# Linear attention's scores and values in blocks of 64 keys, with two heads stacked on the 128 rows

## The chip, the core and the metric

The kernel runs on one core of a Trainium2 chip. The metric is the time of one execution on the device in microseconds (us); a median of several runs is given with its lowest and highest. The profile is one further execution, taken by the hardware profiler.

## The reference, cut to what matters

Eight sequences of 1024 rows and 256 features go through four residual stages: linear attention with its own MLP, an MLP with relu, softmax attention, and an MLP whose operands are rounded to FP4 blocks. All is float32. The change lies in the first stage, for 16 heads of 16 features:

```python
q = sigmoid(heads(Wq, bq)); k = sigmoid(heads(Wk, bk)); v = heads(Wv, bv)
# flows: sink_in, src_comp, sink_alloc, from running sums of q and k
qs = q * (sink_in / normal)[..., None]
vs = v * src_comp[..., None]
kv = cumsum(einsum('bhld,bhlm->bhldm', k, vs), axis=2)
x = einsum('bhld,bhldm->bhlm', qs, kv) * sink_alloc[..., None]
attn = x @ Wo + bo
```

The kernel doesn't form the running sum of outer products for every row. For a chunk of 128 rows it computes, for each head, the scores of all its keys against all its queries, keeps those where the key doesn't come after the query, multiplies them with `vs`, and adds what all earlier chunks give through one 16x16 sum per head, `kv_sum`. Then it adds this chunk's own k times vs to that sum.

## The kernel before, in words

**Groups and chunks.** The rows are 64 chunks of 128 (`P`), four to a group (`G`), 16 groups, two to a sequence. `linear_group` (L970) does a group's layer norms (`front`, L980), and `linear_span` (L1023) its projections to q and k (feature rows by 512 positions), the running sums, and the per-head factors; `comp` holds the factor for v. `linear_chunk` (L1185) does the rest of one chunk: v, scores, values, output projection, layer norm. `dense` (L1388) runs both MLPs a group behind, `soft_chunk` (L1556) the softmax attention and the FP4 MLP, a sequence behind.

**Order of the work.** All of these are generators, run by a small planner (`Plan`, L67). It estimates when every engine and tile would be free (`took`, L164), picks the next part by readiness and priority (`run`, L310), and fixes the order of the instructions on each engine when the program is built. On the chip every engine works through its list in that order and waits on semaphores. `took` prices a matmul by its columns, and at a quarter of that if it uses a 32-row or 32-column tile of the array. Where the planner expects a long pause of TensorE it puts in matmuls of the identity (`fill`, L1710). A transposition (`flip`, L651) goes to TensorE if the planner expects it to have little to do (`idle`, L295), otherwise through a copy on POOL (`cut`), a DMA transpose on SP's queue (`spun`) and a copy on ACT.

**One chunk of linear attention.** The q tile has features on the 128 rows, as two halves k of eight heads. TensorE's array is used as four tiles of 32 rows, r = 0 to 3, with two heads in each, an even and an odd one. ACT makes two copies of the chunk's queries, `qz` (L1233), times `parity[:, e]`, which is 1 on the features of even (e = 0) or odd heads and 0 on the others. A score matmul (L1249) has 128 keys as weights, 32 rows deep, and streams the 256 columns of both copies; there are eight, into four PSUM banks of 512 columns. DVE multiplies each bank by the 0/1 triangle `triu` (L1266) into `sc`; in group 0 (`by_act`), TensorE first puts large negative numbers into the bank from the bf16 tile `later` (L1240), and ACT takes a relu.

For the values (L1306), the weights are 32 columns of `pad`: one of four zeroed tiles `v_pads` (L483), where DVE has written vs with zeros between, so that the 16 columns of one head sit beside 16 zero columns (`v_columns`, L847). Sixteen matmuls stream 128 columns of `sc` each, on four tiles of 32 array columns, and add up in one bank. Ahead of them, from the second chunk of a sequence on, eight matmuls of `kv_sum` with q (L1295) go to the same bank. After them come eight of `kT` with the chunk's vs (L1321), 32 columns each, whose result DVE and POOL add to `kv_sum`.

**Conditions.** The v of chunk c may start when fewer than `V_PADS` = 4 chunks before it are unattended (L1194). The next group's `linear_group` starts when all v's of this group have started (L1000), and each of its fronts when fewer than `RES` = 10 residual tiles are in use (L983). `qz` of chunk c waits until fewer than two chunks before it are unattended (L1226). The next group's q and k wait until this group's four chunks are through the output projection (L1047).

Of the kernel before, what the change touches and what calls it, by code (L numbers as in the profile page):

```python
# [9 lines left out]
F32 = mybir.dt.float32  # L10
# [3 lines left out]
AF = mybir.ActivationFunctionType  # L14
ALU = mybir.AluOpType
AX = mybir.AxisListType

P = 128
D = 256
H = 16  # L20
DH = D // H
FF = 1024
NF = FF // P
INTER = 704
V_PADS = 4
W_FF = 2
IDLE = 1, 0.0
RES = 10
# [4 lines left out]
GT = G * P  # L33
# [12 lines left out]
    "x": (4, D, F32),  # L46
    "n0": (2, D, F32),
    "lin": (4, D, F32),
    "flow": (8, 512, F32),
    "xr": (2, D, F32),  # L50
    "norm": (3, D, F32),
# [15 lines left out]
class Plan:  # L67
# [197 lines left out]
    def pe(self, *tiles, **kw):  # L265
        return self.need("tensor", tiles, **kw)

    def dve(self, *tiles, **kw):
        return self.need("vector", tiles, **kw)

    def act(self, *tiles, **kw):
        return self.need("scalar", tiles, **kw)
# [102 lines left out]
def block_stack_kernel(ctx: ExitStack, tc: tile.TileContext, a: dict, out: bass.AP):  # L375
# [20 lines left out]
    plan = Plan(tc, tc.nc)  # L396
    nc, pe, dve, act, dma = plan, plan.pe, plan.dve, plan.act, plan.dma
    x_dram = a["L0_attn_inputs"]
    B, L, _ = x_dram.shape
# [3 lines left out]
    const = ctx.enter_context(tc.tile_pool(name="const", bufs=1))  # L403
    big = ctx.enter_context(tc.tile_pool(name="big", bufs=1))
    wk = ctx.enter_context(tc.tile_pool(name="wk", bufs=2))
    sm = ctx.enter_context(tc.tile_pool(name="sm", bufs=4))
# [6 lines left out]
    def mm_bank():  # L413
        bank = ps.tile([P, 512], F32, tag="bank", name="bank")
        plan.bank(bank)
        return bank
# [4 lines left out]
    def fresh(kind, need, name=None):  # L421

        need.fresh = kind
        yield need
        return make(kind, name)
# [51 lines left out]
    make_identity(tc.nc, ident)  # L477
    bdiag = const.tile([P, P], F32, name="bdiag")
    make_block_diagonal(tc.nc, bdiag, DH)
    triu = const.tile([P, P], F32, name="triu")  # L480
    make_upper_triangular(tc.nc, triu)

    v_pads = [const.tile([P, H, 32], F32, name=f"v_pad{i}") for i in range(V_PADS)]  # L483
    for v in v_pads:
        nc.vector.memset(v, 0.0)
    neghalf = const.tile([P, 1], F32, name="neghalf")
# [18 lines left out]
    parity = const.tile([P, 2], F32, name="parity")  # L505
# [10 lines left out]
    later = make("q_c", "later")[:, : GT + P]  # L516
# [18 lines left out]
    def late_constants():  # L535
        yield dve(at=0.05)
        nc.vector.tensor_reduce(
            parity, bdiag.rearrange("p (g e d) -> p e g d", e=2, d=DH), AX.XY, ALU.max
        )
        nc.vector.memset(hsum, 0.0)  # L540
        for b in range(4):
            yield dve()
            nc.vector.tensor_copy(
                hsum[:, b, 8 * b : 8 * b + 8], bdiag.rearrange("p (h d) -> p h d", d=DH)[:, :, 0]
            )
        late.add("hsum")
        yield dve(triu)
        nc.vector.tensor_scalar(
            later[:, :GT].rearrange("p (n t) -> p n t", n=4),
            triu.unsqueeze(1).to_broadcast([P, 4, P]),  # L550
            -1.0,
            2.0**100,
            ALU.add,
            ALU.mult,
        )
        yield dve()
        nc.vector.tensor_reduce(
            same[:, 0, :], ident.rearrange("p (t r) -> p r t", r=32), AX.X, ALU.add
        )
        for g in range(NG):  # L560
            yield dve()
            nc.vector.reciprocal(rpos[:, g, :], pos[:, g, :])
        nc.vector.memset(front, 0.0)
        for t in range(1, G):
            yield dve()
            nc.vector.tensor_copy(same[:, t, :], same[:, 0, :])
            nc.vector.tensor_copy(front[: 32 * t, t, :], same[: 32 * t, 0, :])
        late.add("positions")
# [136 lines left out]
    def two(t):  # L705
        return t.rearrange("p (k t) -> p k t", k=2)
# [137 lines left out]
        plan.drop(*turns)  # L844
        weights.add("softmax")

    def v_columns(v, pairs):  # L847

        return bass.AP(
            tensor=v.tensor,  # L850
            offset=v.offset + 64 * pairs.start,
            ap=[list(v.ap[0]), [64, len(pairs)], [64 - DH, 2], [1, DH]],
        )

    weights = set()

# [328 lines left out]
    def linear_chunk(p, i, n0T, comp, qk):  # L1185
# [4 lines left out]
        here = slice(i * P, (i + 1) * P)  # L1190
        yield pe(
            n0T,
            banks=1,
            when=lambda: count["v"] == c and c - count["attended"] < V_PADS and "v" in late,  # L1194
        )
        bank = mm_bank()
        for k in range(2):
            nc.tensor.matmul(
                bank[:, :D],
                lhsT=n0T[:, k, here],  # L1200
                rhs=wqkv[2][:, k, :],
                start=k == 0,
                stop=k == 1,
            )
        count["v"] += 1
        pad = v_pads[c % V_PADS]
        v = yield from fresh("lin", dve(bank), "v")
        nc.vector.tensor_tensor(v, bank[:, :D], bv1, ALU.add)
        yield dve(comp)
        nc.vector.tensor_tensor(  # L1210
            v_columns(pad, range(H // 2)),
            v.rearrange("p (j e d) -> p j e d", e=2, d=DH),
            comp[:, i, H:].rearrange("p (j e) -> p j e", e=2).unsqueeze(3)
            .to_broadcast([P, H // 2, 2, DH]),
# [1 line left out]
        )  # L1216
        plan.drop(v)

        tile_qz = yield from fresh(
            "flow",  # L1220
            act(
                qk[0],
                at=at + 0.62 + 0.06 * i,
                when=lambda: i in groups[p]["scaled"]
                and count["scored"] == c
                and c - count["attended"] < 2,  # L1226
            ),
            "qz",
        )
        count["scored"] += 1  # L1230
        qz = tile_qz.rearrange("p (k e t) -> p k e t", k=2, e=2)
        by_act = p == 0
        for e in range(2):  # L1233
            nc.scalar.activation(
                qz[:, :, e, :], qk[0][:, :, here], AF.Copy, scale=parity[:, e : e + 1]
            )

        yield pe(qz, *([later] if by_act else []), banks=4, tiled=not by_act)
        banks = [mm_bank() for _ in range(4)]
        for bank in banks:  # L1240
            if by_act:
                nc.tensor.matmul(
                    bank, lhsT=later[:, GT:], rhs=later[:, :GT], start=True, stop=False,
                    skip_group_check=True,
                )
        for r, bank in enumerate(banks):
            rows = slice(32 * r, 32 * r + 32)
            for k in range(2):
                nc.tensor.matmul(  # L1249
                    bank[:, k * D : (k + 1) * D],  # L1250
                    lhsT=qk[1][rows, k, here],
                    rhs=qz[rows, k, :, :],
                    start=not by_act,
                    stop=True,
                    skip_group_check=True,
                )
        plan.drop(tile_qz)
        scores = []
        for bank in banks:
            sc = yield from fresh("flow", (act if by_act else dve)(bank), "sc")  # L1260
            sc = sc.rearrange("p (n t) -> p n t", n=4)
            if by_act:
                nc.scalar.activation(sc, bank.rearrange("p (n t) -> p n t", n=4), AF.Relu)
                scores.append(sc)
                continue
            nc.vector.tensor_tensor(  # L1266
                sc,
                bank.rearrange("p (n t) -> p n t", n=4),
                triu.unsqueeze(1).to_broadcast([P, 4, P]),
                ALU.mult,  # L1270
            )
            scores.append(sc)
        end = g == NG - 1 and i == G - 1
        if not end:
# [4 lines left out]
        kv = past.get("kv")  # L1279
        yield pe(  # L1280
            pad,
            *scores,
            *([] if kv is None else [kv]),
            *([] if end else [kT]),
            banks=1,
            tiled=True,
            when=lambda: count["attended"] == c,
        )
        kv = past.get("kv")
# [4 lines left out]
        bank = both[:, :D]  # L1294
        for k in range(2):  # L1295
            for r in range(4):
                if kv is not None:
                    nc.tensor.matmul(
                        bank[32 * r : 32 * r + 32, k * P : (k + 1) * P],
                        lhsT=kv[:, k, 32 * r : 32 * r + 32],  # L1300
                        rhs=qk[0][:, k, here],
                        start=k == 0,
                        stop=False,
                        skip_group_check=True,
                    )
        for k in range(2):  # L1306
            for e in range(2):
                for r in range(4):
                    nc.tensor.matmul(
                        bank[32 * r : 32 * r + 32, k * P : (k + 1) * P],  # L1310
                        lhsT=pad[:, 8 * k + 2 * r + e, :],
                        rhs=scores[r][:, 2 * k + e, :],
                        start=kv is None and k == 0 and e == 0,
                        stop=k == 1 and e == 1,
                        skip_group_check=True,
                    )
        plan.drop(*scores)
        if not end:

            kvbank = both[:, D : D + 64].rearrange("p (k d) -> p k d", k=2)  # L1320
            for k in range(2):  # L1321
                for r in range(4):
                    nc.tensor.matmul(
                        kvbank[32 * r : 32 * r + 32, k, :],
                        lhsT=kT[:, k, 32 * r : 32 * r + 32],
                        rhs=v_columns(pad, range(4 * k + r, 4 * k + r + 1)),
                        start=False,
                        stop=True,
                        skip_group_check=True,
                    )  # L1330
            plan.drop(kT)
        xo = two((yield from fresh("lin", act(bank), "xo")))
        nc.scalar.copy(xo, two(bank))
        if not end:
# [21 lines left out]
        bank = mm_bank()  # L1356
# [8 lines left out]
        h = yield from layernorm_affine("lin", u, ln1g, ln1b)  # L1365
# [398 lines left out]
```

## Time and profile before

| what | value |
| --- | --- |
| median of 3 runs (lowest to highest) | 2563.58 us (2563.43 to 2565.26) |
| the profiled execution's own time | 2562.25 us |
| its span, from the first to the last instruction | 2560.5 us |
| TensorE matmuls busy, share of the span | 2485.7 us, 97% |
| TensorE weight loads busy | 1914.5 us, 75% |
| VectorE (DVE) busy | 2022.4 us, 79% |
| ScalarE (ACT) busy | 1339.4 us, 52% |
| GpSimd (POOL) busy | 1045.1 us, 41% |
| score matmuls (bank<-qz,k) busy, rows | 75.7 us, 1024 |
| value matmuls (bank<-sc,v_pad) busy, rows | 67.9 us, 2048 |

The page of the profile gives busy time by engine and the granted clock; other views give groups of instructions by tile and shape (busy us, mean ns of one, idle before them and who ended it), waits, stretches of time, and a timeline. PE is the matmul row of TensorE, PEld its weight loads. Nearly every instruction stands at line 356, the helper through which the planner issues it, so groups are told apart by their tiles: `out<-in`, rows by elements. A float32 matmul appears as two rows, since the hardware makes two passes. DMA transposes and loads are issued by SP.

### The profile page before, as it was taken

To read this page: it belongs to the slowest core of one execution; us is meant where nothing else is said; L and a number is where in the kernel's file an instruction comes from. 1 tells how busy PE (TensorE), PEld (TensorE's weight loads), DVE (VectorE), ACT (ScalarE), POOL (GpSimd) and SP (SyncE) were. 2 spreads that over 40 slices of the span, in tenths; PEclk is the share of its full clock that TensorE was granted. 3 is DMA by queue.
4 is the path that set the end of the run, shared out by engine and by line. 5 is a ranking of instruction groups with operands and counts; after the bars stand their busy time and mean duration, and the time that the engine had idled before them with its cause. 6 is when DMAs were issued, how large, how long until landed. Compare 5 with 4: busy or idle time off the path is not lost. (4 is left out here: it accounts for less than half of the span.)

```text
span 2560.5 us, 45339 instructions
## 1 busy us (share of the span) xinstructions
PE 2485.7 (97%) x15685; PEld 1914.5 (75%) x15685; DVE 2022.4 (79%) x4416; ACT 1339.4 (52%) x2722; POOL 1045.1 (41%) x1788
## 2 busy tenths in 40 slices
PE   8999999999999999999999999999999999999998
PEld 7777777777877677777777777777777777777767
DVE  6787787887978788796987978688795977866687
ACT  4534546456464645555556564644546456454453
POOL 2433344452534425353453534434443452433222
PEclk9999999999999999999999999999999999999999
DMA  3445555645555554554545554645555444454322
GB/s 88 119 114 148 124 137 126 150 97 125 129 123 133 115 136 108 122 133 110 137 118 121 131 127 120 130 118 120 132 115 119 128 109 116 106 130 117 73 48 62
DMA packets 586821, 301.96 MB, mean 118 GB/s; under 512 B 390240, under 2 KB 575072, under 8 KB 586592
## 3 DMA queue, kind: packets, MB, share of 16 engines
q1 hardware_dynamic: 586592, 299.07, 48.5%
q8 instruction: 124, 2.03, 0.4%
q14 instruction: 105, 0.86, 0.1%
HBM read 188.17 MB, written 20.71 MB: 82 GB/s over the span
## 5 line engine op out<-in xcount | busy, mean ns | idle before, releaser
L356 PE MATMUL bank<-half,w_in 128*128 128x256 f32 x2048 | 531.5, 383 | 14.5 <-ACT half L356 7.0
L356 PE MATMUL bank<-w_out,hidden 128*128 128x256 f32 x2048 | 531.1, 385 | 7.5 <-DMA w_out<-in_L_attn_W_dram 5.0
L356 PEld LDWEIGHTS bank<-w_out,hidden 128*128 128x128 f32 x2048 | 376.0, 191 | 110.7 <-issue 58.2
L356 PEld LDWEIGHTS bank<-half,w_in 128*128 128x128 f32 x2048 | 385.2, 191 | 93.1 <-issue 16.1
L356 POOL TENSOR_SCALAR ln_ve<-ln_mv 128x1 f32<-128x1 f32 x384 | 97.8, 255 | 851.8 <-DVE ln_mv L356 838.5
L356 PE MATMUL bank<-n2T,qT 128*128 128x512 f32 x512 | 243.0, 597 | 5.3 <-ACT qT L356 5.2
L356 POOL TENSOR_TENSOR ln_rstd<-ln_ve,neghalf 128x1 f32<-128x1 f32 x384 | 234.8, 611 | 32.0
L356 ACT ACTIVATE hidden<-bank,c_L_ffn_b 128x256 f32<-128x256 f32 x256 | 120.9, 473 | 241.4 <-PE bank L356 240.6
L356 ACT ACT_TABLE_LOAD x173 | 222.0, 1283 | 25.1 <-DVE nmax L356 19.3
L356 PE MATMUL bank<-vt,probT 128*128 128x256 f32 x1024 | 232.2, 379 | 0.7 <-ACT probT L356 0.7
L356 POOL COPY cut<-prob 128x512 uint16<-128x512 uint16 x211 | 154.5, 751 | 176.7 <-ACT prob L356 110.5
L356 PEld LDWEIGHTS bank<-vt,probT 128*128 128x128 f32 x1024 | 194.0, 190 | 32.3 <-ACT probT L356 2.3
L356 ACT ACTIVATE hidden<-bank,c_L_attn_b 128x256 f32<-128x256 f32 x256 | 119.3, 469 | 168.1 <-PE bank L356 167.7
L356 POOL COPY cut<-n 128x512 uint16<-128x512 uint16 x199 | 146.2, 739 | 121.1 <-DVE n L356 100.4
L356 ACT COPY probT<-spun 128x512 uint16<-128x512 uint16 x223 | 147.4, 675 | 90.6 <-DMA spun<-cut 88.8
L356 PE MATMUL bank<-wgT,xqT 128*128 128x352 f32 x512 | 177.1, 469 | 16.3 <-ACT xqT L356 15.8
L356 PE MATMUL bank<-wdT,hqT 128*128 128x256 f32 x768 | 176.7, 379 | 1.8 <-ACT hqT L356 1.3
L356 PE MATMUL bank<-wuT,xqT 128*128 128x352 f32 x512 | 173.7, 462 | 0.0
L356 PEld LDWEIGHTS bank<-wdT,hqT 128*128 128x128 f32 x768 | 144.9, 190 | 23.3 <-ACT hqT L356 2.1
L356 POOL COPY cut<-hid 128x512 uint16<-128x512 uint16 x156 | 106.9, 707 | 127.7 <-DVE hid L356 93.6
L356 DVE TENSOR_TENSOR sc<-bank,triu 128x512 f32<-128x512 f32 x240 | 149.9, 678 | 8.8 <-PE bank L356 8.6
L356 PEld LDWEIGHTS bank<-n2T,qT 128*128 128x128 f32 x512 | 96.0, 191 | 80.6 <-issue 61.0
(236 smaller groups left out, 4686.8 us busy)
## 6 DMA issues: line engine op xcount, KB each, us to landing
w_in<-in_L_attn_W_dram SPq DMA_DIRECT2D x128, 256.0 KB
w_out<-in_L_attn_W_dram SPq DMA_DIRECT2D x128, 256.0 KB
w_in<-in_L_ffn_w_dram SPq DMA_DIRECT2D x128, 256.0 KB
w_out<-in_L_ffn_w_dram SPq DMA_DIRECT2D x128, 256.0 KB
spread<-packed SPq DMA_DIRECT2D x90, 256.0 KB
spun<-cut SPq DMA_TRANSPOSE x687
x<-in_L_attn_inputs_dram SPq DMA_DIRECT2D x64, 128.0 KB
xr<-in_L_attn_inputs_dram SPq DMA_DIRECT2D x64, 128.0 KB
```

Source lines behind the costliest of these rows:

```text
L356: ins = method(*args, **kw)
```

## The change

The keys of a chunk are cut in two blocks b of 64. The parity mask goes on the keys: ACT writes `kz`, in which the 64 keys of the even head and the same 64 keys of the odd head stand side by side as 128 weight columns. A score matmul streams q itself: all 128 queries for block 0, and the last 64 for block 1, since the first 64 queries come before every key of block 1. So there are 16 score matmuls, of 128 or 64 columns, and a bank holds twice 192 columns instead of 512. The mask `tri` has the same form. The result has two heads' keys on the 128 rows, so vs has to stand likewise in `pad`: DVE writes vs to a tile of its own, `vs`, and POOL and ACT copy it from there in two 64-row pieces each (`into_pad`). Sixteen value matmuls stream 128 or 64 columns. There are two pads instead of four, so L1194's condition becomes fewer than two. The k times vs matmuls read `vs`. Within the score matmuls the loops change order, so that the four row tiles come innermost. The planner's prices for all this follow by its rules, and with them its choices elsewhere.

```diff
@@ -22,7 +22,9 @@
 FF = 1024
 NF = FF // P
 INTER = 704
-V_PADS = 4
+V_PADS = 2
+HB = P // 2
+SCW = P + HB
 W_FF = 2
 IDLE = 1, 0.0
 RES = 10
@@ -46,6 +48,7 @@
     "x": (4, D, F32),
     "n0": (2, D, F32),
     "lin": (4, D, F32),
+    "vs": (V_PADS, D, F32),
     "flow": (8, 512, F32),
     "xr": (2, D, F32),
     "norm": (3, D, F32),
@@ -477,10 +480,16 @@
     make_identity(tc.nc, ident)
     bdiag = const.tile([P, P], F32, name="bdiag")
     make_block_diagonal(tc.nc, bdiag, DH)
-    triu = const.tile([P, P], F32, name="triu")
+    triu = sm.tile([P, P], F32, tag="div", name="triu", bufs=1)
     make_upper_triangular(tc.nc, triu)
-
-    v_pads = [const.tile([P, H, 32], F32, name=f"v_pad{i}") for i in range(V_PADS)]
+    tri = const.tile([P, SCW], F32, name="tri")
+    nc.gpsimd.memset(tri[:, HB:P], 1.0)
+    for e in range(2):
+        h = slice(e * HB, (e + 1) * HB)
+        for c0 in (0, P):
+            nc.gpsimd.tensor_copy(tri[h, c0 : c0 + HB], triu[h, h])
+
+    v_pads = [const.tile([P, 2, H // 2, 32], F32, name=f"v_pad{i}") for i in range(V_PADS)]
     for v in v_pads:
         nc.vector.memset(v, 0.0)
     neghalf = const.tile([P, 1], F32, name="neghalf")
@@ -544,10 +553,10 @@
                 hsum[:, b, 8 * b : 8 * b + 8], bdiag.rearrange("p (h d) -> p h d", d=DH)[:, :, 0]
             )
         late.add("hsum")
-        yield dve(triu)
+        yield dve(tri)
         nc.vector.tensor_scalar(
-            later[:, :GT].rearrange("p (n t) -> p n t", n=4),
-            triu.unsqueeze(1).to_broadcast([P, 4, P]),
+            later[:, : 2 * SCW].rearrange("p (k n) -> p k n", k=2),
+            tri.unsqueeze(1).to_broadcast([P, 2, SCW]),
             -1.0,
             2.0**100,
             ALU.add,
@@ -844,13 +853,9 @@
         plan.drop(*turns)
         weights.add("softmax")
 
-    def v_columns(v, pairs):
-
-        return bass.AP(
-            tensor=v.tensor,
-            offset=v.offset + 64 * pairs.start,
-            ap=[list(v.ap[0]), [64, len(pairs)], [64 - DH, 2], [1, DH]],
-        )
+    def pair_columns(v, j):
+
+        return v.rearrange("p (e j d) -> p j e d", e=2, d=DH)[:, j]
 
     weights = set()
 
@@ -1206,9 +1211,9 @@
         pad = v_pads[c % V_PADS]
         v = yield from fresh("lin", dve(bank), "v")
         nc.vector.tensor_tensor(v, bank[:, :D], bv1, ALU.add)
-        yield dve(comp)
+        vs = yield from fresh("vs", dve(comp))
         nc.vector.tensor_tensor(
-            v_columns(pad, range(H // 2)),
+            vs.rearrange("p (e j d) -> p j e d", e=2, d=DH),
             v.rearrange("p (j e d) -> p j e d", e=2, d=DH),
             comp[:, i, H:].rearrange("p (j e) -> p j e", e=2).unsqueeze(3)
             .to_broadcast([P, H // 2, 2, DH]),
@@ -1216,59 +1221,76 @@
         )
         plan.drop(v)
 
-        tile_qz = yield from fresh(
+        def into_pad(copy, e, b):
+            copy(
+                pad[e * HB : (e + 1) * HB, b, :, e * DH : (e + 1) * DH],
+                vs[b * HB : (b + 1) * HB, e * P : (e + 1) * P].rearrange(
+                    "p (j d) -> p j d", d=DH
+                ),
+            )
+
+        yield plan.pool(vs)
+        for e in range(2):
+            into_pad(nc.gpsimd.tensor_copy, e, e)
+        yield act(vs)
+        for e in range(2):
+            into_pad(nc.scalar.copy, e, 1 - e)
+
+        tile_kz = yield from fresh(
             "flow",
             act(
-                qk[0],
+                qk[1],
                 at=at + 0.62 + 0.06 * i,
                 when=lambda: i in groups[p]["scaled"]
                 and count["scored"] == c
                 and c - count["attended"] < 2,
             ),
-            "qz",
+            "kz",
         )
         count["scored"] += 1
-        qz = tile_qz.rearrange("p (k e t) -> p k e t", k=2, e=2)
+        kz = tile_kz.rearrange("p (k b e t) -> p k b e t", k=2, b=2, e=2)
         by_act = p == 0
         for e in range(2):
             nc.scalar.activation(
-                qz[:, :, e, :], qk[0][:, :, here], AF.Copy, scale=parity[:, e : e + 1]
+                kz[:, :, :, e, :],
+                qk[1][:, :, here].rearrange("p k (b t) -> p k b t", b=2),
+                AF.Copy,
+                scale=parity[:, e : e + 1],
             )
-
-        yield pe(qz, *([later] if by_act else []), banks=4, tiled=not by_act)
-        banks = [mm_bank() for _ in range(4)]
+        kz = tile_kz.rearrange("p (k b n) -> p k b n", k=2, b=2)
+
+        yield pe(tile_kz, qk[0], *([later] if by_act else []), banks=4, tiled=not by_act)
+        banks = [mm_bank()[:, : 2 * SCW] for _ in range(4)]
         for bank in banks:
             if by_act:
                 nc.tensor.matmul(
-                    bank, lhsT=later[:, GT:], rhs=later[:, :GT], start=True, stop=False,
+                    bank, lhsT=later[:, GT:], rhs=later[:, : 2 * SCW], start=True, stop=False,
                     skip_group_check=True,
                 )
-        for r, bank in enumerate(banks):
-            rows = slice(32 * r, 32 * r + 32)
-            for k in range(2):
-                nc.tensor.matmul(
-                    bank[:, k * D : (k + 1) * D],
-                    lhsT=qk[1][rows, k, here],
-                    rhs=qz[rows, k, :, :],
-                    start=not by_act,
-                    stop=True,
-                    skip_group_check=True,
-                )
-        plan.drop(tile_qz)
+        for k in range(2):
+            for b in range(2):
+                for r, bank in enumerate(banks):
+                    rows = slice(32 * r, 32 * r + 32)
+                    nc.tensor.matmul(
+                        bank[:, k * SCW + b * P : k * SCW + P + b * HB],
+                        lhsT=kz[rows, k, b, :],
+                        rhs=qk[0][rows, k, i * P + b * HB : (i + 1) * P],
+                        start=not by_act,
+                        stop=True,
+                        skip_group_check=True,
+                    )
+        plan.drop(tile_kz)
         scores = []
         for bank in banks:
             sc = yield from fresh("flow", (act if by_act else dve)(bank), "sc")
-            sc = sc.rearrange("p (n t) -> p n t", n=4)
+            sc = sc[:, : 2 * SCW].rearrange("p (k n) -> p k n", k=2)
+            bank = bank.rearrange("p (k n) -> p k n", k=2)
             if by_act:
-                nc.scalar.activation(sc, bank.rearrange("p (n t) -> p n t", n=4), AF.Relu)
-                scores.append(sc)
-                continue
-            nc.vector.tensor_tensor(
-                sc,
-                bank.rearrange("p (n t) -> p n t", n=4),
-                triu.unsqueeze(1).to_broadcast([P, 4, P]),
-                ALU.mult,
-            )
+                nc.scalar.activation(sc, bank, AF.Relu)
+            else:
+                nc.vector.tensor_tensor(
+                    sc, bank, tri.unsqueeze(1).to_broadcast([P, 2, SCW]), ALU.mult
+                )
             scores.append(sc)
         end = g == NG - 1 and i == G - 1
         if not end:
@@ -1279,6 +1301,7 @@
         kv = past.get("kv")
         yield pe(
             pad,
+            vs,
             *scores,
             *([] if kv is None else [kv]),
             *([] if end else [kT]),
@@ -1304,14 +1327,14 @@
                         skip_group_check=True,
                     )
         for k in range(2):
-            for e in range(2):
+            for b in range(2):
                 for r in range(4):
                     nc.tensor.matmul(
-                        bank[32 * r : 32 * r + 32, k * P : (k + 1) * P],
-                        lhsT=pad[:, 8 * k + 2 * r + e, :],
-                        rhs=scores[r][:, 2 * k + e, :],
-                        start=kv is None and k == 0 and e == 0,
-                        stop=k == 1 and e == 1,
+                        bank[32 * r : 32 * r + 32, k * P + b * HB : (k + 1) * P],
+                        lhsT=pad[:, b, 4 * k + r, :],
+                        rhs=scores[r][:, k, b * P : P + b * HB],
+                        start=kv is None and k == 0 and b == 0,
+                        stop=k == 1 and b == 1,
                         skip_group_check=True,
                     )
         plan.drop(*scores)
@@ -1323,12 +1346,13 @@
                     nc.tensor.matmul(
                         kvbank[32 * r : 32 * r + 32, k, :],
                         lhsT=kT[:, k, 32 * r : 32 * r + 32],
-                        rhs=v_columns(pad, range(4 * k + r, 4 * k + r + 1)),
+                        rhs=pair_columns(vs, 4 * k + r),
                         start=False,
                         stop=True,
                         skip_group_check=True,
                     )
             plan.drop(kT)
+        plan.drop(vs)
         xo = two((yield from fresh("lin", act(bank), "xo")))
         nc.scalar.copy(xo, two(bank))
         if not end:
```

## The prediction, made before the result was known

> **What bounds the kernel now.** I read the page first: busy time by engine and the granted clock.
>
> ```profile
> PE 2485.7 (97%) x15685; PEld 1914.5 (75%) x15685; DVE 2022.4 (79%) x4416; ACT 1339.4 (52%) x2722; POOL 1045.1 (41%) x1788
> PEclk9999999999999999999999999999999999999999
> ```
>
> TensorE's matmul row is busy 2485.7 of 2560.5 us, at full clock: 74.8 us are idle. Busy can flatter (ends are modelled), so next the table by stretches and the waits.
>
> ```profile
> 0.00:320.00 320.00, 295.06 (x2346) 236.41 (x2347) 242.03 (x574) 148.70 (x342) 110.16 (x207) 0.98 0.44 119
> 320.00:2240.00 1920.00, 1878.35 (x11984) 1441.64 (x11983) 1550.28 (x3322) 1037.04 (x2062) 837.88 (x1412) 1.00 0.52 123
> 2380.00:2560.00 180.00, 172.59 (x757) 126.29 (x755) 141.60 (x319) 83.12 (x180) 46.42 (x80) 1.00 0.28 60
> ```
> ```profile
> ACT hidden L356 <- PE bank L356: 408.3, 253, 8.3
> PE bank L356 <- ACT xqT L356: 15.8, 10, 5.1
> ```
>
> Columns of the first are PE, PEld, DVE, ACT, POOL. PE is full in every stretch, the tail included. The others wait for PE by the hundred us; PE's largest named wait is 15.8 us. So the end is set by the sum of PE's work in its fixed order, and a saved PE microsecond counts unless it becomes a wait. PE by shapes gives the two groups that are recut, and the timeline what one chunk of each costs, start to start:
>
> ```profile
> L356 PE MATMUL bank<-qz,k 32*128 32x256 f32 x1024 | 75.7, 400 | 0.9 <-DVE res L356 0.9
> L356 PE MATMUL bank<-sc,v_pad 128*32 128x128 f32 x2048 | 67.9, 273 | 0.0
> ```
> ```profile
> 824.66 1.03 PE L356 MATMUL bank<-half,w_in 128*128 128x256 f32 x4
> 825.62 1.17 PE L356 MATMUL bank<-qz,k 32*128 32x256 f32 x16
> 826.72 1.13 PE L356 MATMUL bank<-wo,xo 128*128 128x256 f32 x4
> ...
> 838.80 1.06 PE L356 MATMUL bank<-sc,v_pad 128*32 128x128 f32 x32
> 839.68 0.31 PE L356 MATMUL bank<-v_pad,k 128*32 128x32 f32 x16
> ...
> 853.02 1.03 PE L356 MATMUL bank<-half,w_in 128*128 128x256 f32 x4
> 853.88 1.05 PE L356 MATMUL bank<-n2T,wqk 128*128 128x128 f32 x8
> 854.78 0.38 PE L356 MATMUL bank<-ident,h 128*128 128x128 f32 x2
> 854.99 1.03 PE L356 MATMUL bank<-w_out,hidden 128*128 128x256 f32 x4
> ```
>
> Every f32 matmul is two passes, so rows are twice the code's matmuls. Four passes of 256 columns take 853.88 - 853.02 = 0.86 us: 0.216 a pass, 0.84 ns a column. Scores of a chunk: 16 passes in 1.10 us. They run four at a time, one per 32-row tile, so four waves of 0.216 = 0.86, and 0.24 fixed. Values: 32 passes on four 32-column tiles, eight waves in 839.68 - 838.80 = 0.88: 0.109 a wave, the stream of 128 columns. A pass with 128 weight columns and 128 streamed ones takes (854.78 - 853.88)/8 = 0.112.
>
> **What the Trainium skill says.** "TensorE: Matmul & The Clock Gate", section "LDWEIGHTS (loading the stationary operand)": a load costs its columns over 1.2, in ns, whatever the rows; "A 32×128 weight load takes the same time as a 128×128 weight load". That is 107 ns for 128 columns. The trace agrees: in the score group at 825.62 the second load of a tile starts 109 ns after its first, at 32 rows. The same page, "The mechanism", says loads overlap running matmuls "only when row_grp differs". The trace differs: within one row tile the next load starts 1.6 ns after a matmul starts and waves still follow at 0.216, the stream alone. But just one load is ahead at a time. "TensorEngine Tiling (Array Packing)", "Key Properties": a change of tiling mode drains the array. It agrees: 824.66 + 4 x 0.216 = 825.52, the scores start at 825.62, and their first wave still waits 0.11 for its load: some 0.20 us a switch.
>
> **The change part by part.** There are 64 chunks.
>
> **Values** (before L1306): of eight waves four keep 128 columns and four get 64. Loads are 32 columns, about 27 ns, and stay hidden. A 64-column wave isn't in the trace: 0.054 by stream; the N=32 waves at 839.68 run 31 ns apart against 27 of stream, so up to 0.062. I take 0.056: 4 x (0.109 - 0.056) = 0.212, times 64 = -13.6 us (ends -12.0 and -14.1).
>
> **Scores** (L1246): a quarter of the columns goes, but keys are now the weights in 64-key blocks: 16 matmuls instead of 8, eight waves, each behind a fresh load of 128 columns. With one load ahead, a wave costs the longer of load and stream. For 128 streamed columns that is 0.112 by the row above; for 64 the stream is 0.054 and the load, still 0.11, decides. Eight waves of 0.112, the last needing only its stream, are 0.84 against 0.86: -0.03, times 64 = -1.8 us. The weight load eats the saving. This shape is in no trace, so both ends: if loads hid wholly, 4 x 0.108 + 4 x 0.056 = 0.66, -0.21 a chunk, -13 us. If load and stream added up, 4 x 0.22 + 4 x 0.16 = 1.5, +0.65, +42 us. I exclude that end: four loads of 107 ns already lie inside each wave of 0.216 today, and the second four start 13 ns apart, so tiles load side by side. I keep up to 0.13 a wave: +0.15 x 64 = +9 us.
>
> **Constants**: the bf16 seed matmuls of group 0 shrink 512 to 384 columns: 16 x 0.05 = -0.9 us. Four small POOL copies and one memset for the new mask fall in the 1.4 us in which POOL waits before its first ln_ve; two memsets of 0.49 leave the start of DVE. Nil; uncovered, under 1 us.
>
> **What the planner moves.** New costs reorder the list, so I compared the issue orders. Flips taken by PE rather than DMA fall from 274 transposes to 222: -52 x 0.11 = -5.7 us. They become 26 more DMA transposes on SP (687 to 713), 26 more cut copies of about 0.74 on POOL (+19 us) and as many evictions of 0.675 instead of 0.37 on ACT (+8). Dummy matmuls that fill planned pauses rise from 178 to 206: +28 x 0.22 = +6.1. Entries and exits of tiled mode rise from 292 to 308: +16 x 0.20 = +3.2.
>
> **Other engines.** DVE, ACT and POOL are covered by PE's 97% while their waits stay elsewhere:
>
> ```profile
> L356 DVE TENSOR_TENSOR sc<-bank,triu 128x512 f32<-128x512 f32 x240 | 149.9, 678 | 8.8 <-PE bank L356 8.6
> L356 ACT COPY comp<-bank 128x128 f32<-128x128 f32 x15 | 4.0, 264 | 16.1 <-PE bank L356 16.0
> L356 POOL COPY kv_sum<-kv 128x256 f32<-128x256 f32 x8 | 3.4, 428 | 45.5 <-DVE kv L356 45.5
> ```
>
> DVE's mask multiply loses 128 of 512 columns: about -0.13 x 240 = -32 us. The parity copy keeps 256 elements on ACT. Added: two pad copies of 64x128 a chunk on each of ACT (about 0.26, +34 us in all) and POOL (below 0.43, above 0.2; +26 to +55). In ACT's queue the evictions of `hidden` and the kz copies stand behind a pad copy that waits for vs; in POOL's the ln_rstd pairs and cut copies. PE has two `hidden` in hand (LAG), which covers 0.5 us.
>
> **The new wait.** Two pads instead of four: the third and fourth v of a group can start only when chunk c-2 is attended, and the next group's layer norms start after the fourth v. Take the group at 1427 us: v's at 1426 to 1429, chunks attended at 1442, 1448, 1465, 1476. The fourth v would move to about 1448. The next group's statistics stand at 1432, 1432, 1466, 1468, the last two already late for residual buffers, and its q and k follow at 1494. So the two early ones move into a gap of 34 us: nil there. In the order before and after, each group's first k projection stands behind the same amount of PE work, within some 20 us.
>
> **Sum**: -13.6 - 1.8 - 0.9 - 5.7 + 6.1 + 3.2 = -12.7 us. From the profiled execution's 2562.25 (span 2560.5, 1.75 around it) that gives 2549.6; the median of the runs is 1.3 us higher, 2563.58, so 2551.
>
> **Rivals.** (1) Loads hide and scores shrink with their columns: 11 us more, 2540. For it: loads run in all tiles at once. Against: 0.112, not 0.108, where load equals stream today, and one load ahead. (2) The saved time is hidden: PE waits on the other engines instead, about 12 us on 74.8 of idle, 2563. For it: idle in the first 320 us is 25 us, and the new order plans more fill just there. Against: DVE, the fullest other engine, loses 32 us. (3) Slower: the late v's chain stands open. Chunks three and four of 16 groups, 32 in all, must now do v matmul 0.86, bias 0.41, scale 0.47 and pad copies 0.53 before their kz: 2.3 us each, 73 us in all. If a third shows as PE idle, +24: 2575. It decides from 12.7/32 = 0.4 us open per late chunk. Against: PE has dense and softmax work queued, and by the order just 222 flips found PE free. That the change doesn't do what it says is no rival: the order shows the recut matmuls.
>
> **How the numbers follow.** Forecast 0.57, rival 1 0.10, rival 2 0.18, rival 3 0.15. The measurement can tell about 0.2%, 5.1 us. Forecast and rival 1 are faster by more, rival 2 within; a few hundredths of the forecast (waves at 0.13, idle a few us up) fall into no change, so faster 0.65, same 0.20, slower 0.15. The range goes from 2534 (rival 1 with a few us less idle thanks to DVE) to 2567 (rival 2 with some idle more), leaving rival 3 and slivers out.
>
> **What would show it.** Right: values near 0.66 us a chunk start to start, score waves near 0.11 with PEld showing 2048 loads, score group near 1.1 us, PE busy down about 13 us at unchanged idle. Wrong: score waves near 0.06 (rival 1); idle above 85 us (rival 2); idle above 95 us with PE or PEld waiting for kz or v_pad (rival 3).

## The result, and the profile after

| what | before | after |
| --- | --- | --- |
| median (lowest to highest) of 6 runs each on one chip | 2563.51 us (2557.04 to 2565.26) | 2541.41 us (2538.17 to 2544.07) |
| ratio to before, 95% interval | | 0.9914 (0.9904 to 0.9925) |
| the profiled execution's own time, its span | 2562.25, 2560.5 us | 2542.89, 2541.2 us |

The kernel is 22 us faster. The forecast of 2551 us had the direction and about half of the size; its range, 2534 to 2567 us, holds the result. The medians of before differ a little between later sets of runs (2557.64, 2558.01 and 2560.53 us), so each experiment below is given as a ratio to before in its own set.

The page of the changed kernel, busy time by engine and the granted clock:

```profile
PE 2469.1 (97%) x16713; PEld 1919.0 (76%) x16713; DVE 1995.0 (79%) x4414; ACT 1376.0 (54%) x2842; POOL 1089.1 (43%) x1947
PEclk9999999999999999999999999999999999999999
```

PE's busy time fell by 16.6 us (2485.7 to 2469.1), its idle time by 2.7 (74.8 to 72.1). DVE lost 27 us; ACT gained 37 and POOL 44. So PE is still nearly full, in each of the three stretches (after the stretch and its length, the columns are PE, PEld, DVE, ACT, POOL, the granted clock, the DMA share and GB/s). In the first 320 us its idle time rose by 5.4 us; from 320 to 2240 us it fell by 6.0:

```profile
0.00:320.00 320.00, 289.70 (x2539) 236.78 (x2540) 233.92 (x565) 150.17 (x356) 115.58 (x233) 0.98 0.44 114
320.00:2240.00 1920.00, 1884.40 (x12897) 1458.91 (x12896) 1541.98 (x3356) 1073.20 (x2176) 875.22 (x1543) 1.00 0.53 126
2380.00:2541.20 161.20, 156.06 (x683) 115.12 (x681) 132.11 (x294) 76.74 (x161) 50.41 (x82) 1.00 0.32 67
```

The groups by shape have a trap. Columns after the bar: busy us, mean ns of one.

```profile
L359 PE MATMUL bank<-q,kz 32*128 32x128 f32 x1024 | 62.4, 309 | 3.0 <-DVE q L359 1.9 <-DVE rows L359 1.0
L359 PE MATMUL bank<-sc,v_pad 128*32 128x128 f32 x1024 | 47.0, 273 | 0.0
L359 PE MATMUL bank<-q,kz 32*128 32x64 f32 x1024 | 45.8, 244 | 0.0
L359 PE MATMUL bank<-sc,v_pad 128*32 128x64 f32 x1024 | 37.7, 219 | 0.0
```

These four sum to 192.9 us, where before's two rows had 75.7 + 67.9 = 143.6: the recut groups seem 49 us dearer. They aren't. The record of one matmul lasts 219 to 309 ns, while waves of matmuls start 0.056 to 0.21 us apart. So records of the two shapes overlap, and the same microsecond is counted in both rows. What a group costs PE is read from its start to the start of what follows. The timeline of a chunk's values and of a chunk's scores:

```profile
827.01 0.84 PE L359 MATMUL bank<-sc,v_pad 128*32 128x128 f32 x32
827.67 0.31 PE L359 MATMUL bank<-vs,k 128*32 128x32 f32 x16
...
833.28 1.12 PE L359 MATMUL bank<-q,kz 32*128 32x128 f32 x32
834.34 1.13 PE L359 MATMUL bank<-wo,xo 128*128 128x256 f32 x4
```

Values take 827.67 - 827.01 = 0.66 us; before it was 0.88. Scores take 834.34 - 833.28 = 1.06; before it was 1.10. Over all chunks the medians are 0.660 against 0.874 and 1.050 against 1.096; summed from start to next start, values fell from 57.4 to 44.3 us and scores, with their waits, from 72.4 to 71.4. The weight loads of a score group start in eight waves, 0.108 to 0.112 us apart in the trace, and the waves that stream 64 columns are no shorter than those that stream 128.

The groups on the other engines that the change touches, and two waits (us in total, times, longest):

```profile
L359 DVE TENSOR_TENSOR sc<-bank,tri 128x384 f32<-128x384 f32 x240 | 117.1, 546 | 6.5 <-PE bank L359 5.8
L359 ACT COPY v_pad<-vs 64x128 f32<-64x128 f32 x128 | 38.0, 297 | 43.4 <-DVE vs L359 42.0
L359 POOL COPY v_pad<-vs 64x128 f32<-64x128 f32 x128 | 40.9, 320 | 54.7 <-DVE vs L359 47.2 <-DVE q_c L359 2.5 <-PE bank L359 0.8
```
```profile
ACT hidden L359 <- PE bank L359: 328.6, 240, 7.4
PE bank L359 <- ACT xqT L359: 9.8, 9, 2.1
```

The mask multiply lost 0.132 us in each of 240. The pad copies cost 79 us of two engines. ACT still waits for PE by the hundred us (408.3 before), and the weight loads' waits for `kz` and `v_pad` are 1.4 and 1.0 us in all.

### The profile page after: what moved, and what is told of

It reads as the page before. It is cut to its first block, busy times and chain, and to the rows that moved or that the text cites. A ratio compares the mean times of both kernels' runs of the same rounds, so it can differ in the third digit from the quotient of the medians.

```text
span 2541.2 us, 47871 instructions
## 1 busy us (share of the span) xinstructions
PE 2469.1 (97%) x16713; PEld 1919.0 (76%) x16713; DVE 1995.0 (79%) x4414; ACT 1376.0 (54%) x2842; POOL 1089.1 (43%) x1947
## 4 chain that ended last, share of the span: by engine, by line
PE 67%; DVE 17%; DMA 6%; ACT 5%; POOL 3%; issue 2%; SPq 1%; DVEq 0%; POOLq 0%; ACTq 0%
PE bank L359 67%; DMA spun<-cut 4%; DVE hid L359 2%; DVE n L359 2%; ACT L359 2%; DVE prod L359 2%; DVE ln_st L359 1%; DVE u L359 1%; POOL ln_rstd L359 1%; DMA spread<-packed 1%; DVE sc L359 1%; SPq L359 1%; DVE res L359 1%; DVE mx L359 1%; DVE ln_mv L359 1%
## 5 line engine op out<-in xcount | busy, mean ns | idle before, releaser
L359 POOL COPY cut<-prob 128x512 uint16<-128x512 uint16 x211 | 143.2, 702 | 176.3 <-ACT prob L359 124.6
L359 ACT COPY probT<-spun 128x512 uint16<-128x512 uint16 x241 | 158.6, 675 | 85.0 <-DMA spun<-cut 82.0
L359 POOL COPY cut<-n 128x512 uint16<-128x512 uint16 x200 | 138.5, 698 | 129.2 <-DVE n L359 108.2
L359 ACT COPY hqT<-spun 128x512 uint16<-128x512 uint16 x173 | 114.2, 675 | 64.7 <-DMA spun<-cut 64.4
```

Source lines behind the costliest of these rows:

```text
L359: ins = method(*args, **kw)
```

## The experiments

Several readings of the 22 us were open. Theory A is that of the prediction's sum: PE is the bound, every microsecond taken from PE's list comes off the time, and all else is covered. (The prediction allowed that a saved microsecond may become a wait, but its sum has no such term.) Against it stood that DVE's relief matters (B), that the rest comes from the order in which the planner lists the work (C), and the prediction's rivals. Except where the text says so, the order of issue was held: added instructions were hidden from the planner, and those with another shape were priced as in the changed kernel. In the traces the groups of matmuls then follow each other as in the changed kernel.

**The changed kernel once more**, beside the next runs:

> The changed kernel once more, as the measure for the others of this call: ratio to before 0.991 to 0.994.

It took 2538.99 us, 0.9932 (0.9919 to 0.9944) of before: 17 us here. Its page differs from the first by noise, with idle time of 68.8 us:

```profile
PE 2468.7 (97%) x16713; PEld 1918.7 (76%) x16713; DVE 1994.6 (79%) x4414; ACT 1376.3 (54%) x2842; POOL 1089.4 (43%) x1947
```

**DVE made longer.** One small operation follows each mask multiply, and the planner doesn't see it (`size_as = 0`).

```diff
                     sc, bank, tri.unsqueeze(1).to_broadcast([P, 2, SCW]), ALU.mult
                 )
+                nc.size_as = 0
+                nc.vector.tensor_scalar(small([P, 1], "extra", 2), one, 1.0, None, ALU.mult)
+                nc.size_as = None
```

> The changed kernel with one DVE instruction of one element a row (about 0.15 us) behind each of the 240 mask multiplies, unseen by the planner, so that the order on every engine stays that of the changed kernel. DVE gets back the 36 us that the narrower multiply saved it; PE's work is the same. If the gain is PE's own work and the luck of the order, the time stays at 2541 us within 4 (ratio 0.991 to before). If DVE's relief is what shortened PE's waits, the time goes up by 6 us or more, to 2547 or above (ratio 0.9937 or above).

2539.46 us, 0.9933 (0.9919 to 0.9947), with 12 us more on DVE (2007.1 against 1994.6): the same as the changed kernel. The 36 us that were meant became 12, less than half of the 27 us that DVE lost. So 12 us of DVE's work are covered, which speaks against B; at the full size B wasn't tested.

**Score matmuls of block 1 at 128 columns.** They stream their 64 queries twice, the second time into columns that nobody reads; `qs` is the block's queries.

```diff
-    bank[:, k * SCW + b * P : k * SCW + P + b * HB],
+    bank[:, k, b * P : b * P + P],
...
-    rhs=qk[0][rows, k, i * P + b * HB : (i + 1) * P],
+    rhs=qs.unsqueeze(1).to_broadcast([32, 2, HB]) if b else qs,
```

> The changed kernel, but the score matmuls of key block 1 stream their 64 queries twice, 128 columns; mask and values read the same 384 columns as before, and the order on every engine is that of the changed kernel. If a score wave is set by its weight load, waves stay 0.112 us, the score group stays near 1.05 us, and the time stays 2541 within 4 (ratio 0.991). If the streamed columns set it, four waves a chunk grow by 0.054: 64 x 0.21 = +14, 2555 (ratio 0.9967).

2540.55 us, 0.9933 (0.9921 to 0.9946): no change. The timeline of the same chunk:

```profile
829.95 1.17 PE L363 MATMUL bank<-q,kz 32*128 32x128 f32 x32
831.05 1.13 PE L363 MATMUL bank<-wo,xo 128*128 128x256 f32 x4
```

1.10 us instead of 1.06. Over all chunks the group takes 1.103 instead of 1.050: 0.053 more, about one wave's 64 more columns, and so the longer stream of the last wave alone. In the trace of this chunk the eight waves of loads still start 0.109 to 0.112 us apart. Doubling the columns of half the waves costs nothing in the others, so their weight loads set the pace. That is the prediction's step on the scores, and rival 1 falls.

**Value matmuls of block 1 at 128 columns**, by the same means:

```diff
-    bank[32 * r : 32 * r + 32, k * P + b * HB : (k + 1) * P],
+    out_,
     lhsT=pad[:, b, 4 * k + r, :],
-    rhs=scores[r][:, k, b * P : P + b * HB],
+    rhs=sc,
```

When b is 1, `sc` is the block's 64 columns taken twice, and `out_` is 64 columns in each half of the same bank; the second half's aren't read.

> The changed kernel, but the value matmuls of key block 1 stream their 64 columns twice, the second copy into unused columns of the bank; same order on every engine. By the sum for the values (four waves of 0.109 in place of 0.056, 64 chunks) it gives all of their gain back: +13.6, 2555 us (ratio 0.9967). If the values' gain had been hidden by waits, the time stays at 2541.

2547.06 us, 0.9965 (0.9953 to 0.9977).

```profile
828.74 1.06 PE L363 MATMUL bank<-sc,v_pad 128*32 128x128 f32 x32
829.61 0.31 PE L363 MATMUL bank<-vs,k 128*32 128x32 f32 x16
```

The group is back at 0.87 us; over all chunks that is 13.4 us of PE work. The time rose by 0.0033 (give or take 0.0017), 8.5 us. Not all of the work counted.

**Value matmuls of block 1 left out.** The planner still counts them. The values of each chunk's second key block are missing from the result.

```diff
+    if b:
+        plan.took("tensor", "matmul", (out_,), dict(lhsT=left, rhs=right))
+        continue
```

> The changed kernel without the value matmuls of key block 1 (eight of sixteen a chunk), so a part of the values is left out; the planner still counts them, so the order on every engine is that of the changed kernel. It takes 4 x 0.056 = 0.22 us a chunk off PE, 14 us in all. If a microsecond of PE's work counts fully, as in my sum: 14 us below the changed kernel, ratio about 0.988 where that has 0.993. If about half of it becomes waits, as the values at 128 columns hint (13.4 us of work, 7 to 8 us of time), 7 us: ratio 0.9905.

2533.02 us, 0.9899 (0.9886 to 0.9912): 0.0033 less than the changed kernel, 8.5 us, for 14.2 us of work gone. Its page shows 74.2 us of its span of 2533.6 idle on PE:

```profile
PE 2459.4 (97%) x15689; PEld 1906.5 (75%) x15689; DVE 1990.6 (79%) x4414; ACT 1375.7 (54%) x2842; POOL 1087.2 (43%) x1947
```

The two together span 27.6 us of PE work and 0.0066 (give or take 0.0018) of the time, 17 us: 0.6 us of time for 1 us of PE work at a fixed order, between about 0.45 and 0.8. This is where theory A's "every microsecond" fails. The granted clock, below, has a part in it.

**Scores in 32x64 tiles.** If the load of 128 weight columns sets the pace, two tiles with 64 weight columns each should load in half the time.

```diff
+    for e in range(2):
+        half = slice(e * HB, (e + 1) * HB)
...
-            bank[:, k * SCW + b * P : k * SCW + P + b * HB],
-            lhsT=kz[rows, k, b, :],
+            bank[half, k * SCW + b * P : k * SCW + P + b * HB],
+            lhsT=kz[rows, k, b, half],
```

> The changed kernel with each score matmul cut in two along its weight columns: 64 columns of the even head to the array's left half, 64 of the odd head to the right, so eight tiles of 32x64; same order and planned prices. If a load costs its columns and both halves load side by side, block 0 waves stay at 0.109 and block 1 waves fall to about 0.06: 64 x 0.2 = -13, 2528 us (ratio 0.986). If the two halves of a row group share one load path or one stream, waves stay at 0.11 or grow, and the time is 2541 to 2590.

2541.0 us, 0.994 (0.9927 to 0.9953): no gain.

```profile
832.24 1.10 PE L363 MATMUL bank<-q,kz 32*64 32x128 f32 x64
833.27 1.13 PE L363 MATMUL bank<-wo,xo 128*128 128x256 f32 x4
```

The group takes 1.03 us, where 0.85 or so was hoped for. In the trace the first half goes as the theory wants: waves at 832.402, 832.511, 832.567 and 832.625, so 0.11, then 0.056 and 0.058. From the 17th matmul on, starts stand unevenly, typically 16 ns apart instead of 6.7, which eats what the first half gained. In the first half, then, 64 weight columns allow waves of half the length; no run here tells what holds the second half back.

**Before with two pads**, which is the new wait alone:

```diff
-V_PADS = 4
+V_PADS = 2
```

> The kernel before with two pads instead of four and nothing else, so only the condition of v changes (the planner orders anew). If the late start of the third and fourth v is covered, the time is that of before within 0.4%, the spread that I expect of any new order. If the chain stands open (0.4 us or more for each of 32 chunks), it is 13 us slower or more, ratio 1.005 or above.

2557.52 us, 1.0005 (0.9997 to 1.0013). The planner obeys the condition, so this order is a new one too (239 fillers in its list instead of 178), and a few us either way can be the order's, as the last experiments show. But the 24 us of rival 3 aren't there, and the waits of the changed kernel don't show them either. The changed kernel with four pads wasn't tried, and this run had a higher granted clock (below).

**Pad copies twice.** POOL and ACT each do their two pad copies again, unseen by the planner.

```diff
-        for e in range(2):
-            into_pad(nc.gpsimd.tensor_copy, e, e)
+        for n in range(2):
+            for e in range(2):
+                into_pad(nc.gpsimd.tensor_copy, e, e)
+            nc.size_as = 0
+        nc.size_as = None
...
```

> The changed kernel with the pad copies on POOL and ACT made twice, the second time unseen by the planner, order unchanged: +38 us of ACT, +41 us of POOL. If PE's work covers them, as I costed them, the time stays within 3 us of the changed kernel (ratio 0.993); if evictions and kz copies behind them are late, 5 us or more above it (0.995 or above).

2551.47 us, 0.9965 (0.9952 to 0.9979): 0.0033 more than the changed kernel (give or take 0.0018), 8.5 us. Its page:

```profile
PE 2469.9 (97%) x16713; PEld 1919.8 (75%) x16713; DVE 1994.7 (78%) x4414; ACT 1412.9 (55%) x2970; POOL 1124.0 (44%) x2075
```

PE has the same work; its profiled span is 8.4 us longer (2545.9 against 2537.5), with idle time up from 68.8 to 76.0. Counted from each matmul's start to the next one's, the added time stands mostly after the MLP's `half,w_in` matmuls (+4.6 us), the transpositions (+3.8) and `w_out` (+1.7), whose matmuls don't read the pads. It fits that these wait for what ACT and POOL make behind the added copies in their queues. Engines that are busy 54% and 43% of the span were not covered. Both were loaded at once, so the run doesn't say which of the two costs the time.

**Another order for both kernels.** A change of 1% in the planner's price per matmul column changes no instruction of the computation, but the order in which the planner lists them, the transpositions that go to TensorE, and the filler matmuls.

```diff
-            cost = size * (0.853e-3 if op == "transpose" else 1.687e-3)
+            cost = size * (0.853e-3 if op == "transpose" else 1.704e-3)
```

The same edit in before and in the changed kernel:

> The kernel before with one price of the planner, that of a matmul's column, 1% higher, 1.704 instead of 1.687: the work is the same, only the order and what it brings (fills, flips, changes of mode) differ. It measures the luck of the order. If that can carry the part of the gain that my sum over the recut matmuls does not hold, some 4 to 9 us, the time differs from before by such an amount; if orders differ by less than 0.1%, the rest of the gain has another cause.

> The changed kernel with the same price 1% higher. As for the kernel before with it: a difference of 4 to 9 us from the changed kernel either way says that the order's luck is as large as the unexplained part; values and score groups keep 0.66 and 1.05 us a chunk.

And the price 1% lower, 1.670e-3:

> The kernel before with the planner's price of a matmul column 1% lower, 1.670: a third order of the same work. The two so far differ by 8 us; I expect this one in or near that spread, 2545 to 2565, with PE busy within 6 us of the other two.

> The changed kernel with the planner's price 1% lower: a third order. It has 279 fill matmuls against 206 and 200, so more waits are planned; 2538 to 2555. Over three orders each, the mean gain of the change should be that of its work, 8 to 17 us.

| order | before, ratio (95%) | changed, ratio (95%) | gain of the change |
| --- | --- | --- | --- |
| price as it is | 1 | 0.9932 (0.9919 to 0.9944) | 17 us |
| 1% up | 0.9965 (0.9953 to 0.9978) | 0.9973 (0.9960 to 0.9987) | -2 us |
| 1% down | 1.0046 (1.0028 to 1.0065) | 1.0000 (0.9991 to 1.0008) | 12 us |

The busy rows of the four pages, in the order before up, changed up, before down, changed down:

```profile
PE 2488.4 (98%) x15757; PEld 1921.2 (75%) x15757; DVE 2011.8 (79%) x4416; ACT 1353.1 (53%) x2737; POOL 1023.4 (40%) x1808
```
```profile
PE 2472.9 (97%) x16721; PEld 1922.2 (75%) x16721; DVE 1990.9 (78%) x4414; ACT 1365.5 (54%) x2836; POOL 1076.4 (42%) x1937
```
```profile
PE 2503.2 (97%) x15775; PEld 1925.2 (75%) x15775; DVE 2019.7 (78%) x4416; ACT 1327.7 (52%) x2710; POOL 1040.1 (40%) x1786
```
```profile
PE 2489.0 (97%) x16887; PEld 1938.8 (76%) x16887; DVE 1992.7 (78%) x4414; ACT 1350.3 (53%) x2822; POOL 1081.1 (42%) x1933
```

In each pair the change takes 14 to 17 us off PE's busy time (2485.7 to 2469.1, 2488.4 to 2472.9, 2503.2 to 2489.0). That part is steady. The time is not: the same kernel moves by 21 us (before) or 17 us (changed) between three orders. With the price up, before has 234 fillers in its list where it had 178, and is 9 us faster, so more fillers need not mean more time. And the old kernel under the better order, 0.9965, has half of the changed kernel's gain with no change to its attention at all. No run here beat the changed kernel in its own order; those with DVE longer and with 128-column scores equal it within their intervals, and the one below it leaves work out. Two of these expectations missed: with the price 1% down, before took 2570.9 us where 2565 was the upper end, with PE busy for 17.5 us more than in its own order where 6 was the most, and the changed kernel took 2560.58 where 2555 was.

**The granted clock** differs between these runs, and the ratios above aren't corrected for it. The traces show stretches of 3.4 or 6.8 us at half clock: about 24 us in all in the first profile of either kernel, so some 12 us lost and a mean of 0.995. Over 145 runs, each compared with the mean of its own kernel's set, 0.001 less clock goes with 2.4 us more time (give or take 0.3). The means of the runs:

| order | before, mean clock | changed, mean clock | difference, at 2.4 us per 0.001 |
| --- | --- | --- | --- |
| price as it is | 0.9957 | 0.9943 | 3 us |
| 1% up | 0.9960 | 0.9940 | 5 us |
| 1% down | 0.9965 | 0.9945 | 5 us |

By this estimate the change would gain 21, 3 and 17 us at an equal clock, 13 in the mean, while the orders of one kernel would still differ by some 20 us. The same estimate bears on two experiments. Of the 10.6 us of PE work that didn't count, some 5 go with the clock: 0.9932 with the values of block 1 left out, against 0.9954 in before beside it, and 0.9956 against 0.9959 with these at 128 columns. And before with two pads ran at 0.9985; at the 0.9957 of before it would be some 7 us slower, still far from 24. Why the clock is lower in some kernels and orders, no run shows.

## Why the prediction was right, and where it was not

**PE sets the end: right.** 97% before and after; the idle time stayed near 70 us. The page's row of nines was read as full clock; it hides the stretches at half clock.

**Values: right.** -13.6 us was worked out, the starts show 57.4 - 44.3 = 13.1. The term was a 64-column wave at 0.056 us, and a chunk takes the 0.66 us that were forecast.

**Scores: right in mechanism, small in size.** Each wave takes the longer of its load and its stream. The Trainium skill ("TensorE: Matmul & The Clock Gate", "LDWEIGHTS (loading the stationary operand)") has a load of 32 rows cost what one of 128 rows costs, and this case's eight loads at 0.111 us agree. The gain is 0.046 us a chunk instead of 0.03, -2.9 us instead of -1.8 (the prediction's own waves, 0.838 against 0.864, give -1.7). It fits that with the row tiles innermost their starts stand 6.7 ns apart instead of 13.3; no run changes the loop order alone. With their waits, the summed times fell by 1.0 us only.

**DVE, and the new wait, at nothing: right as far as tested** (0.9933 with 12 us more on DVE; 1.0005 with two pads, or some 7 us more at an equal clock, within what a new order scatters).

**"A saved PE microsecond counts": mis-sized.** At a fixed order about 0.6 of it counts (27.6 us of work, 17 us of time). Some 5 us of the rest go with the lower clock, and with the values of block 1 left out PE's idle time is 74.2 us where the changed kernel has 68.8. The three recut groups, 13.1 + 2.9 and the 0.9 forecast for the seeds, make 17 us of work and so only some 10 us of time.

**ACT and POOL "covered by PE's 97%": failed.** The pad copies were put at nil. Doubling them costs some 8.5 us, for 71 us more of busy time on the two pages (ACT 36.6, POOL 34.6). If the first set costs as much, which no run shows, nearly all of those 10 us are paid back.

**"What the planner moves": failed.** Flips -5.7, fillers +6.1 and switches +3.2 were added up as if each instruction in the list were time. From start to next start, the trace gives fillers +15.1 (45.5 to 60.6) and the transpositions of activations -3.3, while groups that nobody touched fell: `n2T,wqk` by 6.4, `wdT` 3.7, `half,w_in` 3.7, `w_out` 3.3 us. A new order moves pauses from one group to another, and three orders of one kernel lie up to 21 us apart. Counting its instructions doesn't say which way it goes.

So the sum, -12.7 us against -22 and -17, fell short although two of its terms were too hopeful: work counted in full, copies counted at nothing. What it lacked is what the order brought. By the runs, the recut itself is worth between 10 us (copies free) and about 2 us (copies at 8.5); the mean gain over the three pairs is 9 us or 0.35% (13 by the estimate at an equal clock). It lies near the upper end, though three orders that scatter so leave it uncertain by several us. The rest of the 17 to 22 us, 7 to 20 us, is put down to the order. That is a difference, not a cause traced: which placement in the list gives it stays open.

**Rivals.** Rival 1 gave the nearest time, 2540, for a reason that the run with 128-column scores refutes: that was luck. Rival 2, saved time turned into pauses, holds in part, in the 0.4 that didn't count; its sign, idle time above 85 us, didn't come. Rival 3 is refuted: the changed kernel is faster, and its waits for `kz` and `v_pad` come to 2.4 us.

## What to carry to other kernels

Price a matmul on array tiles by the longer of its weight columns and its streamed columns: here the cut below 128 streamed columns paid for the values (32 weight columns) and not for the scores (128). Test what lies "under cover" by doubling it, whatever its engine's busy share. Where a planner fixes the order, run both kernels under several orders before crediting a change with less than that scatter, here about 20 us. And compare the clocks of the runs: here 0.002 of it was worth some 5 us.

## What the runs showed that was not expected

- Score matmuls on four row tiles start 6.7 ns apart when the tiles alternate, and 13.3 ns when two matmuls of one tile are neighbours in the list.
- In a burst of f32 matmuls with 64-column weights, starts go from 6.7 to typically 16 ns apart after the 16th matmul, that is after about 64 loads and passes. The cause is open.
- PE's busy row isn't its work: the old kernel under the 1% lower price shows 2503.2 us against 2485.7, with 43 more fillers of about 0.22 us (9.5 us) in its list. The fillers explain some half of it. The row's ends are modelled, so it may count pauses as work; no run separates that.
